# ScalarE loads column addresses in three places of a step (12, 8 and 8, then 12, 8 and 12); the first nodes' words come in parts, and the tail goes by tiles

## The chip, the cores and the metric

The kernel runs on one NeuronCore of a Trainium2 chip. The core has five engines that run their own instruction streams and wait for each other through semaphores: TensorE (PE; its weight loads are listed as PEld), VectorE (DVE), ScalarE (ACT), GpSimd (POOL) and SyncE (SP). Sixteen DMA engines move data; transfers are issued by POOL (here the gathers, with an index per partition), SP and ACT. The metric is the device time of one execution in microseconds (us), as the median of several runs.

## The reference

One message-passing layer of a graph network over 12,500 nodes of 128 numbers and 412,500 edges sorted by destination. Cut to what matters:

```python
f0, f1 = x0 @ W1_0e, einsum(x1, W1_1o)      # scaled; halves: features and self part
e0, e1 = feat0[src], feat1[src]             # 128 numbers of the source node, per edge
h = gelu(gelu(edge_attr_8 @ W_mlp1) @ W_mlp2)
w00, w01, w10, w11 = h @ Wp_00, h @ Wp_01, h @ Wp_10, h @ Wp_11
mid0 = [w00 * e0 * ea0,  w11 * sum(e1 * ea1)]
mid1 = [(w01 * e0) x ea1,  w10 * e1 * ea0]
n0, n1 = segment_sum(mid0, dst), segment_sum(mid1, dst)
y = c * self + s * [n0 @ W2_0e, n1 @ W2_1o]
out = layernorm(x + y)
```

## The kernel before

**Tiling.** The edges are cut into 806 runs of 512 (`SB`), one run to a step `s`; a run has four quarters of 128 edges (`Q`), one edge to a partition. Four steps are a chunk `c` (202 chunks). The nodes are cut into 25 groups of 512 (`GN`, the last has 212 nodes, in tiles of 128 and 84).

**Start** (the loop over `b`). x is loaded group by group (SP, tile `own`), turned by PE and copied by ACT into `xT` (x with the node number along the free axis, kept in SBUF), multiplied by `wf` and stored by ACT's queue to `table` in DRAM: `table` holds every node's features. The list `weight_loads()` is issued by SP, one entry in each turn of this loop from b = 5 on; before the change its last entries are `first_node` (the first destination of each chunk) and the tiles `tile_first` (shown as `tf` in the trace: the first destination of each of the 16 quarters of a chunk, 4-byte words, one row for each chunk; 128 rows in the first tile and 74 in the second, whose last row is loaded apart). `tile_places` (DVE) turns these words into byte offsets, which `places(c)` loads into PE's registers. After the loop SP issues `aid_load()`, up to 12 entries a step: the source numbers of the columns that are picked or aided (tiles `pick` and `aid_at`).

**A step.** The features of the 512 source nodes come into `G[s]` in three ways. Most quarters are fetched by POOL with one gather of 128 rows each (`gather`, L222). The last quarter of every 14th run is fetched by SP with 128 single-row transfers (`aid`). One quarter of some runs is *picked*: DVE or ACT copies 128 single columns out of `xT` into a tile `gt`, each copy with a column address out of a register (L190 on DVE, L192 on ACT), PE multiplies `gt` by `wf` (L198) and ACT writes the result into `G` (L199). How many columns an engine picks in a step, and in which places of the step, is the table `SLOTS`: DVE 12 and 12, with 0, 8, 8 or 16 more; ACT 12 and 16. `pick_nodes(e, s, slot)` loads that many addresses into registers (TENSOR_LOAD, L178), and `pick(e, n)` issues the copies of addresses that were loaded earlier. 172 quarters are picked by ACT, 197 by DVE and 56 are aided; POOL is left with 2,798 gathers, of which the first 72 read x itself.

With the edge weights `w` (PE, from the two-layer MLP whose gelus run on ACT, L540 and L556, in the odd steps of a chunk, two chunks ahead), DVE forms the messages `M` (L637 once and L641 twice a step), and PE sums them by destination with the one-hot tiles `own` (L666, L668) into `sums`. DVE adds `sums` to `acc` after each chunk (`add`). `select(c)` (DVE, ahead of each chunk) builds `own` and reads one value of each gathered quarter into `SEEN` (L597), so that DVE waits there for the gathers.

**Groups of nodes.** When all edges of a group are in `acc`, `moments` (PE L698 and L701, copy by ACT L706) computes its output rows, `statistics` (DVE, L714) their mean and variance, `normalise` (ACT L742) the result, and SP stores it. The last full group (`before_last`) falls due near the end, the last group after the last chunk.

**Order.** PE, ACT, DVE and SP run their instructions in the order in which the program writes them; POOL's gathers stand in the order of the steps. `G` has 19 buffers (`LEAD`), so a gather may be issued up to 18 steps ahead of its use. The transfers of SP and ACT take turns on eight semaphores; a transfer waits until the one before it on its semaphore has landed.

Of the kernel before, what the change touches and what calls it, by code (L numbers as in the profile page):

```python
# [21 lines left out]
P = 128  # L22
# [27 lines left out]
STEPS = 12  # L50
SLOTS = {DVE: [(12, 12, 0), (12, 12, 8), (12, 12, 8), (12, 12, 16)], ACT: [(12, 16)]}
COL_Q = {DVE: Q - 2, ACT: Q - 3}
COL_FROM = {DVE: 12, ACT: 12}
LNB = 2
TURN_AT = (7, 9, 11, 13, 15, 17, 18, 20, 22, 24)


@with_exitstack
def gnn_kernel(ctx: ExitStack, tc: tile.TileContext, x, src, dst, ea4, ea8, w1_0, w1_1, wm1, wm2,
# [277 lines left out]
    def weight_loads():  # L337

        yield w1r, sub(wm1, 0, [[0, P // RAD], [HID, RAD], [1, HID]])
        yield w2b, sub(wm2, 0, [[0, 2], [HID, HID], [1, HID]])  # L340
        for j, w in enumerate((wp00, wp01, wp10, wp11)):
            yield wpb[:, j * MUL:(j + 1) * MUL], sub(w, 0, [[0, 2], [MUL, HID], [1, MUL]])
        for t, w in ((w20, w2_0), (w21, w2_1)):
            yield t[:MUL, :], w[:MUL, :]
            yield t[MUL:, :], sub(w, MUL * MUL, [[0, 3], [MUL, MUL], [1, MUL]])
        yield first_node, sub(dst, 0, [[1, 1], [CH * SB, NCH]])
        for b, t in enumerate(tile_first):
            c0, n = b * P, t.shape[0]
            last = c0 + n == NCH and E < NCH * CH * SB
            if last:  # L350
                yield (t[n - 1:n, :].rearrange("a (k o) -> a k o", o=1),
                       sub(dst, (NCH - 1) * CH * SB, [[1, 1], [0, CH * Q], [1, 1]]))
                k = -(-(E - (NCH - 1) * CH * SB) // P)
                yield t[n - 1:n, :k], sub(dst, (NCH - 1) * CH * SB, [[k * P, 1], [P, k]])
            yield t[:n - last], sub(dst, c0 * CH * SB, [[CH * SB, n - last], [P, CH * Q]])

# [35 lines left out]
    first_at = cst.tile([1, NCH], I32)  # L392
    NT = -(-NCH // P)
    tile_first = [cst.tile([min(P, NCH - b * P), CH * Q], I32, name=f"tf{b}") for b in range(NT)]
# [12 lines left out]

    def tile_places():

        for b, t in enumerate(tile_first):  # L410
# [234 lines left out]
    def places(c):  # L645

        b, r = divmod(c, P)
        _, PLACE[c] = nc.values_load_multi_w_load_instructions(
# [35 lines left out]
    pend, done = [], []  # L684
    before_last = due[NCH - 1][0] - 1

    def moments(b, sums=None):
        n0, nn, full, tail, tiles = group(b)
        if not pend:
            Y["y"] = wk.tile([P, LNB, XB, P], F32, name="y", bufs=1)  # L690
            Y["v"] = wk.tile([P, LNB * XB, 2], F32, name="mv")
            nc.vector.memset(Y["v"], 1.0)
        j = len(pend)
        pend.append(b)
        pt = ps.tile([P, XB, P], F32, name="h")
        at = n0 - base[-1] if b in due[NCH - 1] else 0
        for t, k in tiles:
# [5 lines left out]
            else:  # L703
                nc.vector.tensor_tensor(pt[:k, t, :], pt[:k, t, :], sums[:k, t, :], op=OP.add)
        if full:
            nc.scalar.activation(Y["y"][:, j, :full, :], pt[:, :full, :], AF.Copy)  # L706
        if tail:
            nc.scalar.activation(Y["y"][:tail, j, full, :], pt[:tail, full, :], AF.Copy)

    def statistics(b):  # L710
        j = pend.index(b)
        st = wk.tile([P, XB, 6], F32, name="bst")
        for t, k in group(b)[4]:
            nc.vector.bn_stats(st[:k, t, :], Y["y"][:k, j, t, :])  # L714
            nc.vector.bn_aggr(Y["v"][:k, j * XB + t, :], st[:k, t, :])
# [7 lines left out]
    def normalise(last=False, keep=False):  # L723
# [9 lines left out]
        for j, b in enumerate(pend):  # L733
            if b in done:
                continue
            for t, k in group(b)[4]:
                i = j * XB + t - i0
                if last and t % 2:
                    nc.vector.tensor_scalar(y[:k, j, t, :], y[:k, j, t, :], r[:k, i:i + 1], m[:k, i:i + 1],
                                            op0=OP.mult, op1=OP.add)  # L740
                    continue
                nc.scalar.activation(y[:k, j, t, :], y[:k, j, t, :], AF.Identity,  # L742
                                     bias=m[:k, i:i + 1], scale=r[:k, i:i + 1])
            store_nodes(nc.sync, out, b, y[:, j])
        done[:] = pend if keep else []
# [3 lines left out]
    def norm(bs):  # L749
        for b in bs:  # L750
            moments(b)
            move_sums()
# [13 lines left out]
    def norm_last(bs):  # L766
# [6 lines left out]
        if len(pend) > len(done):  # L773
            deviations()
            normalise(True)

    odd_f = cst.tile([1, 1], F32)
# [118 lines left out]
    with tc.manual_schedule(engines={PE, ACT, DVE, SP}):  # L896
# [7 lines left out]
        for b in range(min(AHEAD, NG)):  # L904
# [41 lines left out]
        for s in range(NCH * CH + CH):  # L946
# [120 lines left out]
```

## Time and profile before

| | us |
|---|---|
| median of 3 runs (3550.64 to 3557.92) | 3552.09 |
| profiled execution, its own time | 3556.29 |
| its span in the profile | 3554.4 |

| engine | busy us | share of the span |
|---|---|---|
| PE | 3159.9 | 89% |
| DVE | 3129.2 | 88% |
| ACT | 2797.6 | 79% |
| POOL | 2667.6 | 75% |

The profile page gives the busy time of each engine, the chain of work that ended last, and groups of instructions by source line with the idle time ahead of them and what ended it. Busy time leaves out what an engine's sequencer does: address loads, semaphore waits and the issue of transfers (rows marked ACTq, DVEq, SPq). "issue" as the end of an idle stretch means that nothing else in the profile ended it. A row of the windows view gives a stretch of the span, its length, and then busy time and count of the chosen instructions in it.

### The profile page before, as it was taken

What the parts mean: (1) busy time and instruction counts of PE and PEld (TensorE: products, weight loads), DVE (VectorE), ACT (ScalarE), POOL (GpSimd) and SP (SyncE); (2) the same over time, 40 slices, a digit from 0 to 9 for tenths busy, and PEclk for the clock granted to TensorE, in tenths of its full rate; (3) what the DMA queues carried; (4) which work ended last, traced back from release to release, by engine and by line L of the source; (5) the groups of instructions that cost most, each with busy time, mean ns of one, the idle gap of its engine ahead of it and who ended that gap; (6) DMA issues with size and microseconds to landing.
All of it is one profiled execution on the core that took longest, in us unless ns stands there. A gap on an engine that the chain in (4) does not pass through costs nothing. (4 is left out here: it accounts for less than half of the span.)

```text
span 3554.4 us, 143693 instructions
## 1 busy us (share of the span) xinstructions
PE 3159.9 (89%) x28598; PEld 2755.6 (78%) x28598; DVE 3129.2 (88%) x29317; ACT 2797.6 (79%) x23671; POOL 2667.6 (75%) x2804
## 2 busy tenths in 40 slices
PE   6899898998898988998899898898899989888888
PEld 6777777787777777877788787787787777777777
DVE  2699999999999999999899899888899888889897
ACT  3488788788888888887887888877787887788785
POOL 7777777777777777777777777777777777777775
PEclk8999999998999999899998899989899999999998
DMA  8322332223322223322323323323323232232221
GB/s 199 70 62 68 63 64 65 63 61 74 64 60 67 63 60 74 64 60 62 68 61 70 67 59 64 65 63 68 65 62 64 59 69 63 60 69 63 60 65 47
DMA packets 579225, 239.29 MB, mean 67 GB/s; under 512 B 483651, under 2 KB 528747, under 8 KB 578347
## 3 DMA queue, kind: packets, MB, share of 16 engines
q0 software_dynamic: 89536, 183.55, 20.3%
q1 hardware_dynamic: 468041, 40.02, 9.1%
q10 hardware_dynamic: 20770, 6.47, 0.8%
q8 instruction: 252, 4.13, 0.5%
q14 instruction: 626, 5.13, 0.5%
HBM read 217.00 MB, written 12.80 MB: 65 GB/s over the span
## 5 line engine op out<-in xcount | busy, mean ns | idle before, releaser
L222 POOL DMA_INDIRECT G<-table,idx x2726 | 2598.9, 953 | 836.7 <-issue 718.5
L192 ACT ACTIVATE gt<-xT 128x1 f32 x22016 | 2166.7, 190 | 73.3 <-issue 53.6
L190 DVE COPY gt<-xT 128x1 f32 x25216 | 1728.6, 144 | 212.1 <-issue 172.9
L666 PE MATMUL sums<-own,M 128*128 128x96 f32 x6446 | 1354.8, 294 | 74.3 <-DVE M L641 73.0
L668 PE MATMUL sums<-own,M 128*128 128x96 f32 x6446 | 1319.7, 288 | 85.1 <-DVE M L641 84.1
L666 PEld LDWEIGHTS sums<-own,M 128*128 128x128 f32 x6446 | 1037.5, 201 | 181.9 <-DVE M L641 101.7
L668 PEld LDWEIGHTS sums<-own,M 128*128 128x128 f32 x6446 | 1035.3, 202 | 108.9 <-DVE M L641 107.6
L641 DVE TENSOR_TENSOR M<-w,G 128x384 f32<-128x384 f32 x1612 | 880.1, 547 | 0.0
L569 PE MATMUL w<-wpb,h 64*128 64x128 f32 x6448 | 649.3, 305 | 57.8 <-DVE M L641 56.3
L569 PEld LDWEIGHTS w<-wpb,h 64*128 64x128 f32 x6448 | 496.5, 197 | 199.6 <-issue 74.3
L637 DVE TENSOR_TENSOR M<-w,G 128x256 f32<-128x256 f32 x806 | 333.4, 414 | 34.4 <-issue 19.9
L540 ACT ACTIVATE h<-h 128x512 f32<-128x512 f32 x404 | 216.3, 586 | 178.6 <-PE h L536 165.7
L536 PE MATMUL h<-eT,w1b 64*128 64x128 f32 x3232 | 288.7, 319 | 8.4 <-ACT e L523 8.3
L536 PEld LDWEIGHTS h<-eT,w1b 64*128 64x128 f32 x3232 | 241.3, 218 | 38.7 <-ACT e L523 13.7
L556 ACT ACTIVATE h<-h 128x512 f32<-128x512 f32 x404 | 213.5, 577 | 26.3 <-PE h L551 22.5
L551 PE MATMUL h<-h,w2b 64*64 64x256 f32 x3232 | 222.6, 391 | 0.0
L199 ACT ACTIVATE G<-h 128x128 f32<-128x128 f32 x369 | 96.4, 277 | 120.5 <-PE h L198 76.4
L198 PE MATMUL h<-wf,gt 128*128 128x128 f32 x738 | 143.5, 294 | 1.9 <-ACT h L556 0.9
L529 ACT ACTIVATE eT<-h 128x128 f32<-128x128 f32 x202 | 56.0, 277 | 112.7 <-PE h L527 89.5
L551 PEld LDWEIGHTS h<-h,w2b 64*64 64x64 f32 x3232 | 104.5, 133 | 44.8 <-issue 0.5
L630 DVE TENSOR_TENSOR own<-oh,e 128x512 f32<-128x512 f32 x202 | 137.6, 681 | 0.7 <-issue 0.2
L681 DVE TENSOR_TENSOR acc<-sums,acc 128x384 f32 x202 | 111.2, 550 | 9.7 <-issue 6.2
(113 smaller groups left out, 1329.1 us busy)
## 6 DMA issues: line engine op xcount, KB each, us to landing
G<-table SPq DMA_DIRECT2D x7168, 0.5 KB
G<-table,idx POOLq DMA_INDIRECT x2726
e<-in_edge_attr SPq DMA_DIRECT2D x201, 64.0 KB
own<-in_x SPq DMA_DIRECT2D x24, 256.0 KB
table<-acc ACTq DMA_DIRECT2D x24, 256.0 KB
xt<-in_edge_attr SPq DMA_DIRECT2D x24, 256.0 KB
out<-y SPq DMA_DIRECT2D x24, 256.0 KB
xt<-in_dst SPq DMA_DIRECT2D x5, 256.0 KB
```

Of the source, the lines that this page charges most:

```text
L190: nc.vector.tensor_copy(to, col)
L192: nc.scalar.activation(to, col, AF.Copy)
L222: nc.gpsimd.indirect_dma_start(out=G[s][:, q, :], out_offset=None, in_=x if s < raw_runs else table, in_offset=bass.IndirectOffsetOnAxis(a ...
L536: nc.tensor.matmul(p1[h][:, j // 2, j % 2, :], w1b[rows, j, :], eT[c][rows, :], start=True, stop=True)
L540: nc.scalar.activation(H1[c][h], p1[h].rearrange("p k j e -> p (k j e)"), AF.Gelu_apprx_tanh, scale=1.0 / math.sqrt(RAD))
L551: nc.tensor.matmul(p2[r][k * HID:(k + 1) * HID, h * n:(h + 1) * n], w2b[rows, :], H1[c][h][rows, k * n:(k + 1) * n], start=True, stop=True)
L556: nc.scalar.activation(H2[c][r].rearrange("p k j e -> p (k j e)"), p2[r], AF.Gelu_apprx_tanh, scale=1.0 / math.sqrt(HID))
L569: nc.tensor.matmul(WP[i][:, q, :], H2[c][q % 2][rows, k, q // 2, :], wpb[rows, :], start=True, stop=True)
L637: nc.vector.tensor_tensor(M[s][:, :, :, :MUL], w[:, :, :2 * MUL].rearrange("p q (a u) -> p q a u", a=2), g[:, :, None, :MUL].to_broadcast( ...
L641: nc.vector.tensor_tensor(M[s][:, :, j, MUL:].rearrange("p q (i u) -> p q i u", i=3), w[:, :, None, (2 + j) * MUL:(3 + j) * MUL].to_broadc ...
L666: nc.tensor.matmul(flat[:, bass.ds(at, 4 * FIRST_HALF)].bitcast(F32), M[s][:, q, 0, :], own[:, 3 * WIDE:], start=False, stop=False)
L668: nc.tensor.matmul(sb[:, 1:, bass.ds(at, 4 * WIDE)].bitcast(F32), M[s][:, q, 1, :], own[:, :3 * WIDE].rearrange("p (a j) -> p a j", a=3), ...
```

## The change

**1. Three places for ACT's addresses.** ACT's row of `SLOTS` becomes (12, 8, 8) in one step and (12, 8, 12) in the next: 28 and 32 columns in turn, 30 on average, in place of 28. The third load stands behind a new `pick` that comes ahead of the gelus of the odd steps. With the larger number of columns 184 quarters are picked by ACT in place of 172, and POOL's gathers from `table` become 2,714 in place of 2,726.

**2. First nodes' words.** `tile_first` becomes three tiles that begin at chunks 0, 16 and 144. `first_node` and the first tile (16 rows) are loaded first in the list of SP; the other two tiles (128 rows, and 58 of which one is loaded apart) are loaded behind the pick rows, after the start loop. `tile_places` runs for the first tile in the start loop and for the other two in step 9.

**3. Tail by tiles.** Of the four tiles of `before_last`, three are computed by `moments` in earlier chunks, as soon as each is complete (`done_at`); `find_first` clamps the offsets of later sums so that they leave these tiles alone. The last group's rows stay in PSUM and are read there by `statistics` and `normalise`, without a copy by ACT, and its two tiles are stored each by its own transfer, one from ACT's queue and one from SP's.

```diff
-SLOTS = {DVE: [(12, 12, 0), (12, 12, 8), (12, 12, 8), (12, 12, 16)], ACT: [(12, 16)]}
+SLOTS = {DVE: [(12, 12, 0), (12, 12, 8), (12, 12, 8), (12, 12, 16)], ACT: [(12, 8, 8), (12, 8, 12)]}
+FIRST_TILES = 16
...
     def weight_loads():
+        yield first_node, sub(dst, 0, [[1, 1], [CH * SB, NCH]])
+        yield from tile_loads(0)
         yield w1r, sub(wm1, 0, [[0, P // RAD], [HID, RAD], [1, HID]])
...
-        yield first_node, sub(dst, 0, [[1, 1], [CH * SB, NCH]])
-        for b, t in enumerate(tile_first):
...
+    def tile_loads(b):
+        t, c0 = tile_first[b], tile_from[b]
+        n = t.shape[0]
...
+        yield t[:n - last], sub(dst, c0 * CH * SB, [[CH * SB, n - last], [P, CH * Q]])
...
+    tile_from = [0, *range(FIRST_TILES, NCH, P)]
...
+    done_at = [math.ceil((before_last * GN + (t + 1) * P + MARGIN) / N * NCH) - 1 for t in range(XB)]
...
     def find_first():
...
+        for t, (a, z) in enumerate(zip(done_at, done_at[1:])):
+            nc.vector.tensor_scalar(strays[:, a + 1:z + 1], strays[:, a + 1:z + 1], float((t + 1) * P), None, op0=OP.max)
...
-    def moments(b, sums=None):
+    def moments(b, sums=None, part=None):
         n0, nn, full, tail, tiles = group(b)
+        if part is not None:
+            tiles = tiles[part:part + 1]
...
+        if sums is None and b == NG - 1:
+            Y["pt"] = pt
+            return
+        if part is not None:
+            nc.scalar.activation(Y["y"][:, j, part, :], pt[:, part, :], AF.Copy)
+            return
...
+    def rows_of(b, j, t, k):
+        return Y["pt"][:k, t, :] if b == NG - 1 and "pt" in Y else Y["y"][:k, j, t, :]
...
+                if last:
+                    eng = nc.sync if t % 2 else nc.scalar
+                    eng.dma_start(out[b * GN + t * P:b * GN + t * P + k, :], y[:k, j, t, :])
...
-            moments(b)
+            moments(b, part=XB - 1 if b == before_last else None)
...
-                 NG // 2 + 9: tile_places, NG // 2 + 10: lambda: mlp2(1), NG // 2 + 11: make_ws, NG: make_wpost}
+                 NG // 2 + 9: lambda: tile_places([0]), NG // 2 + 10: lambda: mlp2(1), NG // 2 + 11: make_ws, NG: make_wpost}
...
-        late = list(aid_load())
+        late = list(aid_load()) + [load for b in range(1, NT) for load in tile_loads(b)]
...
+            pick(ACT, P)
+            pick_nodes(ACT, s, 2)
             if k % 2 and c + 2 < NCH:
-                pick(ACT, P)
                 (mlp1 if k == 1 else mlp2)(c + 2)
...
+            if k == 3 and c - 1 in done_at[:-1]:
+                moments(before_last, part=done_at.index(c - 1))
...
+            if s == 9:
+                tile_places(range(1, NT))
```

On ACT, an odd step and the step after it, in the steady part of the program (`gt` are picked columns, `pick` their addresses, `h` the two halves of a gelu). Before:

```order
L178 TENSOR_LOAD pick_832
L192 ACTIVATE gt_40310<-xT 128x1 x12
L178 TENSOR_LOAD pick_832
L192 ACTIVATE gt_40310<-xT 128x1 x16
L556 ACTIVATE h_40621<-h 128x512
L556 ACTIVATE h_40623<-h 128x512
L178 TENSOR_LOAD pick_832
L192 ACTIVATE gt_40310<-xT 128x1 x12
```

And now, with the change's line numbers (L179 is the load, L193 the copy):

```order
L193 ACTIVATE gt_44344<-xT 128x1 x12
L179 TENSOR_LOAD pick_823
L193 ACTIVATE gt_44344<-xT 128x1 x8
L179 TENSOR_LOAD pick_823
L556 ACTIVATE h_45433<-h 128x512
L556 ACTIVATE h_45435<-h 128x512
L193 ACTIVATE gt_44344<-xT 128x1 x12
L179 TENSOR_LOAD pick_823
```

Ahead of the two gelus of an odd step now stand 20 copies of that step in place of 28, with a load between the copies and the gelus, and 12 copies stand behind them.

On SP, the end of the start loop and the loads behind it (`own` are groups of x, `tf` the first nodes' words, `e` edge attributes). Before:

```order
L925 DMA tf_95<-in_dst 1x16x1
L252 DMA own_75<-in_x 128x128
L254 DMA own_75<-in_x 84x128
L925 DMA tf_95<-in_dst 1x7x1
L925 DMA tf_95<-in_dst 73x16x1
L496 DMA e_828<-in_edge_attr 128x16x8
L959 DMA aid_at<-in_src 56x128
L959 DMA pick_830<-in_src 128x128
L959 DMA pick_831<-in_src 69x128
L959 DMA pick_832<-in_src 19x128 x2
```

And now:

```order
L253 DMA own_75<-in_x 128x128
L255 DMA own_75<-in_x 84x128
L512 DMA e_819<-in_edge_attr 128x16x8
L993 DMA aid_at<-in_src 56x128
L993 DMA pick_821<-in_src 128x128
L993 DMA pick_822<-in_src 69x128
L993 DMA pick_823<-in_src 9x128 x8
L993 DMA pick_823<-in_src 8x128 x7
L993 DMA pick_824<-in_src 4x128 x11
L993 DMA pick_824<-in_src 3x128 x4
L993 DMA tf_95<-in_dst 128x16x1
L993 DMA tf_96<-in_dst 1x16x1
```

The words stand behind the pick rows now, and ACT's pick rows take 30 transfers in place of 14, since the pattern of picked runs repeats less often.

On PE, `before_last` between the last steps (`h` the group's rows, `sums` the messages' sums). Before:

```order
L668 REGISTER_ALU
L668 MATMUL sums<-own_74,M 128x3x32
L698 MATMUL h<-ws,xT 128x128
L701 MATMUL h<-wpost,acc 128x128 x4
L698 MATMUL h<-ws,xT 128x128
L701 MATMUL h<-wpost,acc 128x128 x4
L698 MATMUL h<-ws,xT 128x128
L701 MATMUL h<-wpost,acc 128x128 x4
L698 MATMUL h<-ws,xT 128x128
L701 MATMUL h<-wpost,acc 128x128 x4
L569 MATMUL w<-wpb,h_203822 128x128 x2
```

And now:

```order
L685 REGISTER_ALU
L685 MATMUL sums<-own_74,M 128x3x32
L717 MATMUL h<-ws,xT 128x128
L720 MATMUL h<-wpost,acc 128x128 x4
L585 MATMUL w<-wpb,h_209287 128x128 x2
```

Three of the four tiles have left this place; they stand six, four and two chunks earlier, one at each.

More of the change, by code (lines that the diff above doesn't have):

```diff
@@ L345, in weight_loads @@
             yield t[MUL:, :], sub(w, MUL * MUL, [[0, 3], [MUL, MUL], [1, MUL]])
[L346 to L355 removed]
+    def tile_loads(b):
+        t, c0 = tile_first[b], tile_from[b]
+        n = t.shape[0]
+        last = c0 + n == NCH and E < NCH * CH * SB
+        if last:
+            yield (t[n - 1:n, :].rearrange("a (k o) -> a k o", o=1),
+                   sub(dst, (NCH - 1) * CH * SB, [[1, 1], [0, CH * Q], [1, 1]]))
+            k = -(-(E - (NCH - 1) * CH * SB) // P)
+            yield t[n - 1:n, :k], sub(dst, (NCH - 1) * CH * SB, [[k * P, 1], [P, k]])
+        yield t[:n - last], sub(dst, c0 * CH * SB, [[CH * SB, n - last], [P, CH * Q]])
     def make_w1b():
@@ L392, in gnn_kernel @@
     first_at = cst.tile([1, NCH], I32)
-    NT = -(-NCH // P)
-    tile_first = [cst.tile([min(P, NCH - b * P), CH * Q], I32, name=f"tf{b}") for b in range(NT)]
+    tile_from = [0, *range(FIRST_TILES, NCH, P)]
+    NT = len(tile_from)
+    tile_first = [cst.tile([z - a, CH * Q], I32, name=f"tf{b}")
+                  for b, (a, z) in enumerate(zip(tile_from, tile_from[1:] + [NCH]))]
+    before_last = due[NCH - 1][0] - 1
+    assert len(due[NCH - 1]) == 1
+    done_at = [math.ceil((before_last * GN + (t + 1) * P + MARGIN) / N * NCH) - 1 for t in range(XB)]
+    assert due[done_at[-1]] == [before_last] and done_at == sorted(set(done_at))
+    assert not any(c in due for c in range(done_at[0] - 1, done_at[-1])) and done_at[-1] < NCH - 2
     def find_first():
@@ L406, in find_first, with tile_places @@
         nc.vector.tensor_reduce(odd[0:1, 2 * NB:2 * NB + 1], strays, axis=mybir.AxisListType.X, op=OP.add)
-    def tile_places():
-        for b, t in enumerate(tile_first):
+    def tile_places(bs):
+        for b in bs:
+            t = tile_first[b]
             n = t.shape[0]
@@ L645, in places @@
     def places(c):
-        b, r = divmod(c, P)
+        b = max(b for b, a in enumerate(tile_from) if a <= c)
+        r = c - tile_from[b]
         _, PLACE[c] = nc.values_load_multi_w_load_instructions(
@@ L692, in moments @@
             nc.vector.memset(Y["v"], 1.0)
-        j = len(pend)
-        pend.append(b)
+        if b not in pend:
+            pend.append(b)
+        j = pend.index(b)
         pt = ps.tile([P, XB, P], F32, name="h")
@@ L737, in normalise @@
                 i = j * XB + t - i0
+                z = rows_of(b, j, t, k)
                 if last and t % 2:
-                    nc.vector.tensor_scalar(y[:k, j, t, :], y[:k, j, t, :], r[:k, i:i + 1], m[:k, i:i + 1],
+                    nc.vector.tensor_scalar(y[:k, j, t, :], z, r[:k, i:i + 1], m[:k, i:i + 1],
                                             op0=OP.mult, op1=OP.add)
[L741 to L744, printed above, removed]
+                else:
+                    nc.scalar.activation(y[:k, j, t, :], z, AF.Identity,
+                                         bias=m[:k, i:i + 1], scale=r[:k, i:i + 1])
+                if last:
+                    eng = nc.sync if t % 2 else nc.scalar
+                    eng.dma_start(out[b * GN + t * P:b * GN + t * P + k, :], y[:k, j, t, :])
+            if not last:
+                store_nodes(nc.sync, out, b, y[:, j])
         done[:] = pend if keep else []
```

4 lines of the change are left out of this document (2 added, 2 removed).

## The prediction

> **What bounds the kernel now.** I read the page's groups first, for the engine that never rests, then the windows by steps, then the waits. The page shows GpSimd busy for only 75% of the span, but its row and the list of its first and last gathers tell another story:
>
> ```profile
> L222 POOL DMA_INDIRECT G<-table,idx x2726 | 2598.9, 953 | 836.7 <-issue 718.5
> L222 POOL DMA_INDIRECT G<-in_x,idx_raw x72: 940/944/1091, 3.8 to 92.7; - x72
> L222 POOL DMA_INDIRECT G<-table,idx x2726: 938/944/1508, 99.4 to 3528.3; - x195
> POOL G L222 <- issue: 740.2, 2427, 0.3
> POOL G L222 <- DVE M L641: 50.2, 147, 5.7
> ```
>
> Nearly every gather has 0.3 us ahead of it, whatever is named as its releaser (740.2 over 2427, 50.2 over 147): that gap belongs to the gather. The only long wait is one of 5.7 us near 99 us. GpSimd therefore issues gathers without a pause from 3.8 to 3528.3 us. What the steps do beside it (first the message instruction, one per step; then the gathers):
>
> ```profile
> 100.00:400.00 300.00, 28.69 (x70) 0.95 0.29 63
> 400.00:1900.00 1500.00, 147.27 (x356) 0.94 0.30 64
> 1900.00:3400.00 1500.00, 142.76 (x345) 0.93 0.30 64
> ...
> 400.00:1900.00 1500.00, 1136.18 (x1194) 0.94 0.30 64
> 1900.00:3400.00 1500.00, 1136.45 (x1193) 0.93 0.30 64
> ```
>
> The gathers run at the same pace in both halves: 1500/1194 = 1.256 us each. The steps do not: 1500/356 = 4.213 us, then 1500/345 = 4.348 us. In the first half the other engines use up GpSimd's head start; in the second they run at its heels, and DVE begins to wait for gathers. Of DVE's 45 us of such waits all but 4 lie after 1900 us:
>
> ```profile
> DVE SEEN L597 <- DMA G<-table,idx: 36.8, 32, 2.1
> DVE SEEN L597 <- DMA G<-table: 8.5, 10, 2.6
>   DMA G<-table: 4.1, 4
> ```
>
> (The last row is the part before 1900 us.) So the end is set by the number of gathers, and the other engines have 0.135 us a step in hand. What sets *their* 4.213 us is read between 300 and 1500 us, where they run free:
>
> ```profile
> 300.00:1500.00 1200.00, 1077.69 (x9931) 938.83 (x9930) 1105.93 (x10538) 995.76 (x8576) 909.05 (x955) 0.94 0.30 65
> DVE gt L190 <- issue: 60.3, 175, 0.6
> DVE M L637 <- PE w L569: 0.2, 1, 0.2
> PE sums L668 <- DVE M L641: 24.4, 35, 0.9
> ACT h L540 <- PE h L536: 39.1, 27, 5.6
> ```
>
> DVE is busy for 1105.9 of 1200 us and waits 60.3 us for its own address loads: 97% is its own. It waits for PE's weights once, 0.2 us; PE waits for DVE. ACT is busy for 995.8 us (83%) and mostly waits for PE.
>
> **Part 1, ACT's columns.** Twelve more quarters are picked, so twelve gathers go: 12 x 1.256 = **-15.1 us**, as long as GpSimd stays the bound. The price on ACT is two more copies a step:
>
> ```profile
> L192 ACT ACTIVATE gt<-xT 128x1 f32 x22016 | 2166.7, 190 | 73.3 <-issue 53.6
> L178 ACTq TENSOR_LOAD <-pick x1696: 306/808/1850, 143.9 to 3516.2; - x189
>   issue: 19.7, 84
> ```
>
> A copy costs 2166.7/22016 = 0.098 us, two of them 0.20 us a step, against an idle 0.72 us a step (204.2 of 1200 us, 285 steps). A third address load is sequencer time, 0.8 us as a median for 12 or 16 addresses; between 300 and 1500 us all loads together held ACT up for 19.7 us in 84 places, 0.07 us a step, so half as many again cost about 0.035 us (below: nothing; above: a whole 0.8 us each). ACT ends near 88% busy. None of this is on the path unless DVE comes to wait for PE and PE for ACT. PE does wait for gelus, 25.8 + 14.0 us in that window:
>
> ```profile
> PE h L527 <- ACT h L556: 25.8, 9, 5.4
> PE h L698 <- ACT h L556: 14.0, 8, 2.3
> ```
>
> The new order puts 8 copies fewer (0.79 us) ahead of the gelus in odd steps, which works against these waits. The cover is thin: the new bound gives a step (3509 - 95)/788 = 4.33 us on average over the table gathers, and over the whole run a free step may grow only from 4.213 to 4.25 before the saving shrinks (worked out under the rivals). I take -15.1; the bounds are in the rivals.
>
> **Part 2, first nodes' words.** The 5.7 us wait ahead of the first gather from `table` is named after DVE, but what is late is the table: ACT's last store is issued at 97.05. ACT had stood still for 10 us before:
>
> ```profile
> 71.02 0.60 ACT L295 ACTIVATE xT<-w 128x512 f32<-128x512 f32 x1 [0.26 <-PE w L294]
> 81.27 0.38 ACTq L260 DMA_DIRECT2D table<-acc  x1
> 81.75 1.08 ACT L540 ACTIVATE h<-h 128x512 f32<-128x512 f32 x2 [10.13 <-DMA pick<-in_src]
> 97.05 0.62 ACTq L262 DMA_DIRECT2D table<-acc  x1
> 99.37 0.94 POOL L222 DMA_INDIRECT G<-table,idx  x1 [5.68 <-DVE M L641]
> 65.16 1.58 SPq L925 DMA_DIRECT2D tf<-in_dst  x2
> 66.80 8.94 SPq L496 DMA_DIRECT2D e<-in_edge_attr  x1
> 76.87 11.40 SPq L959 DMA_DIRECT2D pick<-in_src  x16
> q1 hardware_dynamic: 1094, 0.00, 6.7%
> q1 hardware_dynamic: 2295, 0.12, 54.8%
> ```
>
> The store at 81.27 shares a semaphore with a pick load that SP could issue only after the 73 x 16 words: SP's next issue took 8.94 us, while its queue moved 1094 tiny packets in 9.2 us (66.8 to 76 us; the last row is the same queue at 59 to 62 us, where 2295 packets, most of them the words of the 128-row tile, took 3 us). The change takes this load out of the start, so ACT's 9.6 us go: its last store would come at 87.4. But now 33 pick loads stand ahead of the 128-row words, and by the program's semaphores the last two stores follow those. From about 63 us on, 33 x 0.71 us (11.40/16) gives 87, the words land near 91, the last store about 94, the gather at 95 to 96 in place of 99.37: **-4 us**. Bounds: the whole wait gone, -5.7; SP slower by a quarter or the words late, +4.
>
> [...] If the stall had another cause, this term would be nil and the sum -19.6 us.
>
> What goes elsewhere is small: `tile_places` for two tiles is twelve short DVE instructions in step 9, while GpSimd leads by some 16 steps.
>
> **Part 3, the tail.** From the start of the last gather 26 us pass. In them PE does four tiles of `before_last` in a row and DVE waits for the weights behind them:
>
> ```profile
> 3527.97 0.41 PE L698 MATMUL h<-ws,xT 128*128 128x128 f32 x2
> 3531.57 1.06 PE L701 MATMUL h<-wpost,acc 128*128 128x128 f32 x8
> 3532.56 0.71 PE L569 MATMUL w<-wpb,h 64*128 64x128 f32 x7
> 3536.21 0.42 DVE L637 TENSOR_TENSOR M<-w,G 128x256 f32<-128x256 f32 x1 [5.08 <-PE w L569]
> 3546.57 0.29 DVE L714 BATCH_NORM_STATS2 bst<-y 128x6 f32<-128x128 f32 x1 [1.94 <-ACT y L706]
> 3546.40 3.47 SPq L260 DMA_DIRECT2D out<-y  x2
> 3549.97 0.72 SPq L262 DMA_DIRECT2D out<-y  x1
> ```
>
> 3532.56 - 3527.97 = 4.59 us for four tiles; three leave: -3.4. DVE's 5.08 us are longer than that, so all of it counts. The earlier tiles cost PE 1.15 us each at places where it waits anyway. Without ACT's copy the statistics start about 0.5 us earlier, and two queues in place of one save some 0.6 us at the end (the second issue). **-4.5 us**; below -5.5, above -2 if earlier tiles push a step.
>
> **Sum:** -15.1 - 4 - 4.5 = -23.6 us. The profiled span of 3554.4 becomes 3530.8. The median of the runs, 3552.09, lies 2.3 us below that span; I subtract from it: **3528.5 us**.
>
> **Rivals.** (a) *The start gains nothing* because the last stores wait as long for the words behind 33 loads: 3532.5, or 3536.5 with the loss of 4. For it: more loads, same semaphores; against it: ACT's 9.6 us. (b) *ACT's work reaches DVE in part.* 72 steps are done at 400 us (2 before 100, 70 after); the last 734 take x each, and 15 us follow (3539 to 3554), 10.5 after the change. The new span is 400 + 734x + 10.5: it exceeds 3530.8 when x is over 4.251, and 3554.4 when x is over 4.283. With x = 4.263 (0.05 of the 0.20 us arrives): 3539.5, so 3537 as a median. (c) *Slower: ACT becomes the bound's feeder.* If half of the added work arrives at DVE, through late gelus or late picked quarters, x = 4.313: 3576, so **3574**; with all of it 3647. It decides from +0.07 us a step. For it: six times less slack than added work, and 19.7 us of exposed loads already. Against it: DVE waited for the weights for 0.2 us in 285 steps, PE has waits for DVE to give, and gelus come earlier. (d) *The change does not do what it says*: the twelve quarters fall in the free first half. That cannot save less, since the total number of gathers sets the last one.
>
> **Chances.** The forecast 0.65 (own range 3525 to 3534); (a) 0.13; (b) 0.10, half of it faster still and half level with before; (c) 0.12. A measurement of this kernel tells 0.2%, 7 us, from no change. Faster: 0.65 + 0.13 + 0.05 = 0.83; same 0.05; slower 0.12. Eight times in ten the time lies from 3520 to 3546: below the forecast for a start and tail at their bounds and the runs' spread, above it for (a) and most of (b).
>
> **What would show it.** Right: 2,714 gathers from `table` at 1.256 us; the first near 95 us and the last near 3509; steps at 4.2 us, then 4.33, with DVE's waits for gathers beginning later than 1900 us; ACT near 88% busy between 300 and 1500 us; one tile of L698's kind among the last steps and 21.6 us from the start of the last gather to the end. Wrong: a free step above 4.25 us, DVE waiting for `w`, or GpSimd waiting for a buffer by more than 0.3 us, would be (b) or (c); a first table gather at 99 us or later would be (a).

## The result: 66.6 ms in place of 3.55, and where the profile puts it

The changed kernel takes 66,644.89 us (median of 4 runs, 66,607.38 to 66,678.48) where the kernel before took 3555.01 us on the same chip: 18.75 times as long (95% interval 18.72 to 18.78). The forecast was 3528.5 us.

The page of the changed kernel begins like this (a group's columns: line, engine, operation, result and operand, count, then busy us, mean ns, and idle time ahead with what ended it):

```profile
span 66676.7 us, 678515 instructions
...
PEclk9955555555555555555555555555555555555555
...
L859 PE MATMUL h<-ident,g_a 125*8 125x125 f32 x3300 | 1213.9, 368 | 28287.2 <-DMA g_a<-in_edge_attr 28287.2
L918 POOL DMA_INDIRECT sums<-G,g_to x3300 | 3995.2, 1211 | 28442.0 <-DVE G L917 28442.0
...
L223 POOL DMA_INDIRECT G<-table,idx x2714 | 2587.9, 954 | 834.3 <-issue 652.0
```

Read the counts before the times. The 2,714 gathers of the forecast are there, with their 954 ns. The granted clock falls to about half after the first twentieth of the span (9 tenths, then 5), and the costliest groups occur 3,300 times, on lines that the prediction never named: 412,500 edges / 125. They belong to `general()`, the second path of the program, which computes everything again, 125 edges at a time, each pass waiting for its own transfers. The timeline of SP in the changed kernel shows where it starts (start, length, engine, line, transfer):

```profile
3535.15 0.35 SPq L775 DMA_DIRECT2D out<-y  x1
3536.38 21.57 SPq L261 DMA_DIRECT2D sums<-ft  x25
...
3559.78 0.29 SPq L844 DMA_DIRECT2D g_si<-in_src  x1
```

The fast path issues its last store at 3535.15 us, and then the general path begins. That leaves (66,676.7 - 3536.4)/3300 = 19.1 us a pass. The program enters it by this, at its very end:

```python
padded = P - RP if RP else 0                 # 44: empty places in the last quarter
n_odd = nc.values_load(odd_i, ...)           # edges and runs that don't fit the fast path
with tc.If(n_odd > padded):
    general()
```

`n_odd` counts, among others, edges whose destination lies below the first of their quarter, or 8 (`J`) or more above it. From the inputs the kernel before counts 44, the empty places alone, against a limit of 44: there is no margin, and a single odd edge more decides.

What changed the count shows in the transfers into the scratch tile (listed as `acc`), in the view of that tile on SP. Of the kernel before:

```profile
L480 SPq DMA_DIRECT2D acc<-in_dst x1: 659/659/659, 22.3 to 22.3; - x1
...
L925 SPq DMA_DIRECT2D acc<-in_dst x1: 646/646/646, 53.4 to 53.4; - x1
```

Of the changed kernel:

```profile
L496 SPq DMA_DIRECT2D acc<-in_dst x1: 647/647/647, 22.2 to 22.2; - x1
...
L959 SPq DMA_DIRECT2D acc<-in_dst x1: 812/812/812, 28.4 to 28.4; - x1
```

and, from its DVE timeline, the instruction that reads the first of them:

```profile
41.02 0.42 DVE L473 CAST ft<-acc 128x512 f32<-128x512 int32 x1
```

The first transfer brings the destinations of the first 128 runs (512 words a row, run 0 in row 0), the second brings `first_node`: `line(0, I32)`, the first 202 words of row 0 of the same tile. Before, it came at 53.4 us, after the words had been read (at 41.62 us there). Now it comes at 28.4 us and run 0's first 202 words are gone when DVE reads them at 41.02 us. The transfers and the read come in the order in which the program writes them, so this is no race: the program says it so. Counting run 0 again with those words: in its first quarter 127 of 128 are 8 or more above the first; in its second, 73 of 74 likewise, and the 54 that are left now lie below the first. 127 + 73 + 54 = 254, and 44 + 254 = 298 > 44.

### The profile page after: what moved, and what is told of

It is laid out like the page before. It is cut to its first block, busy times and chain, and to the rows that moved or that the text cites. A ratio compares the mean times of both kernels' runs of the same rounds, so it can differ in the third digit from the quotient of the medians.

```text
span 66676.7 us, 678515 instructions
## 1 busy us (share of the span) xinstructions
PE 25039.1 (38%) x101418; PEld 17416.0 (26%) x101418; DVE 17140.9 (26%) x92411; ACT 12800.6 (19%) x45159; POOL 14627.8 (22%) x12693
## 5 line engine op out<-in xcount | busy, mean ns | idle before, releaser
L918 POOL DMA_INDIRECT sums<-G,g_to x3300 | 3995.2, 1211 | 28442.0 <-DVE G L917 28442.0
L856 POOL DMA_INDIRECT G<-table,g_si x3300 | 3980.2, 1206 | 21579.7 <-DMA g_a<-in_edge_attr 20088.8
L894 PE MATMUL h<-wpost,G 128*125 128x128 f32 x26400 | 6834.3, 440 | 1554.0 <-ACT G L891 1554.0
L894 PEld LDWEIGHTS h<-wpost,G 128*125 128x125 f32 x26400 | 5854.0, 327 | 2505.5 <-ACT G L891 2505.5
L889 PE MATMUL w<-ident,G 125*128 125x125 f32 x13200 | 3522.0, 422 | 6216.3 <-DVE G L881 6216.3
L914 POOL DMA_INDIRECT G<-sums,g_di x3300 | 3995.7, 1211 | 1006.4 <-DVE G L876 949.7
L889 PEld LDWEIGHTS w<-ident,G 125*128 125x128 f32 x13200 | 2334.6, 216 | 7095.1 <-issue 7095.1
L877 DVE SCALAR_TENSOR_TENSOR G<-G,g_a 125x32 f32<-125x32 f32 x3300 | 830.8, 252 | 9179.0 <-ACT G L873 9179.0
L905 PE MATMUL h<-G 125*125 125x128 f32 x6600 | 2600.4, 496 | 1209.6 <-ACT G L896 1209.6
L871 PE MATMUL w<-wpb,G 64*125 64x128 f32 x6600 | 2599.2, 496 | 1184.2 <-ACT G L869 1184.2
L885 DVE SCALAR_TENSOR_TENSOR G<-G,g_a 125x32 f32<-125x32 f32 x9900 | 2443.3, 247 | 0.0
L883 DVE SCALAR_TENSOR_TENSOR G<-G,g_a 125x32 f32<-125x32 f32 x9900 | 2442.7, 247 | 0.0
```

What stands on the lines that cost most here:

```text
L856: nc.gpsimd.indirect_dma_start(out=g, out_offset=None, in_=table, in_offset=bass.IndirectOffsetOnAxis(ap=si, axis=0))
L871: nc.tensor.matmul(pw, h2, wpb[:HID, :], start=True, stop=True)
L883: nc.vector.scalar_tensor_tensor(m[:, 1 + k, :MUL], w[:, MUL:2 * MUL], a4[:, 1 + k:2 + k], g[:, :MUL], op0=OP.mult, op1=OP.mult)
L885: nc.vector.scalar_tensor_tensor(m[:, 1 + k, r], w[:, 3 * MUL:], a4[:, 1 + k:2 + k], g[:, r], op0=OP.mult, op1=OP.mult)
L889: nc.tensor.transpose(pm[:, k, :T], m[:, k, :], ident[:T, :T])
L894: nc.tensor.matmul(pc, mt[:, k, :T], wpost[:, k, :], start=k == 0, stop=k == 3)
```

## The experiments: what sets off the general path

The theory is the overwrite, with a count of exactly 298. The rivals: the clamp that part 3 adds to `find_first`, or the split tiles of part 2, raise the count. The four kernels ran on one chip, where the kernel before took 3552.63 us (9 runs, 3551.96 to 3555.68).

**A limit of 298.**

```diff
-    with tc.If(n_odd > padded):
+    with tc.If(n_odd > padded + 254):
```

> The changed kernel with one constant other: the branch into the general path asks whether the count of odd edges and runs exceeds 298 instead of 44. Theory (the overwrite): first_node is now loaded before the destinations of run 0 are read out of the same words, so run 0 has 202 wrong destinations; from the inputs the count is 44 + 54 + 200 = 298, so the branch is not taken and the time is that of the fast path alone: 3540 us (3533 to 3546), 11 to 15 us under the kernel before. Run 0's messages go to wrong nodes here, and nothing repairs them. Rivals (the clamp of the later sums, or the places of the three tiles, is counted as odd): the clamp covers up to 198 chunks and the tiles up to 202 x 16 words, so the count could be any number; over 298 the time is 66.6 ms.

Measured: 3535.77 us (4 runs, 3531.38 to 3541.86), ratio to the kernel before 0.9956 (0.9941 to 0.9971).

**A limit of 297** (`padded + 253`).

> As the run with the limit of 298, but with 297. The overwrite gives a count of exactly 298, so here the general path runs and the time is 66.6 ms. If the count is any other number under 298, both runs are fast; over 298, both slow. Only a count of exactly 298 separates them.

Measured: 66,692.21 us (one run). The count is over 297 and not over 298: exactly the number from the inputs.

**The kernel before with the load moved.**

```diff
     def weight_loads():
+        yield first_node, sub(dst, 0, [[1, 1], [CH * SB, NCH]])
...
-        yield first_node, sub(dst, 0, [[1, 1], [CH * SB, NCH]])
```

> The kernel before, with one line moved: the load of first_node stands first in weight_loads instead of ahead of the tiles. Nothing else of the change is in it: no clamp, two tiles as before, the old tail and SLOTS. The overwrite: 66.6 ms (the fast part of 3.55 ms and 63.1 ms of the general path). The clamp or the tiles as the cause: 3552 us, as before.

Measured: 65,845.94 us (one run), and the general path's groups stand in its page:

```profile
L825 PE MATMUL h<-ident,g_a 125*8 125x125 f32 x3300 | 1214.1, 368 | 27644.8 <-DMA g_a<-in_edge_attr 27644.8
```

One moved line in the kernel before is enough; neither clamp nor split is in it. That its general path is 0.8 ms shorter than the changed kernel's was not followed up.

**The change with other words for `first_node`.**

```diff
-    first_node = line(0, I32)
+    first_node = line(12, I32)
```

> The changed kernel with one constant other: first_node lies in line 12 of the scratch tile, words that no early load writes, instead of line 0. All three parts of the change stay, and the load stays early. The overwrite: the count is 44, the branch is not taken, 3540 us (3533 to 3546). The clamp or the tiles as the cause: still 66.6 ms. Where the time of the fast part goes: first gather from the table near 94 us, GpSimd waits of about 6 us in all at 160 to 190 us, last gather near 3514.6, and 25 us from there to the end. The prediction's own sum (3528.5) would need the waits at 160 to 190 us away and a tail shorter by 4.5 us.

Measured: 3540.59 us (5 runs, 3533.24 to 3541.87), ratio 0.9960 (0.9947 to 0.9974). With everything else of the change in place the general path is gone. The overwrite is the cause, and the clamp and the split are not.

## The experiments: the terms of the sum

This last version, called the mended kernel from here on, is the one that the prediction's sum was about. Its gathers, in the view of their line:

```profile
L223 POOL DMA_INDIRECT G<-table,idx x2714: 940/944/1500, 94.5 to 3507.9; - x194
```

Its windows by DVE's message instruction, one a step:

```profile
400.00:1900.00 1500.00, 148.02 (x357) 0.95 0.28 64
1900.00:3400.00 1500.00, 144.22 (x348) 0.94 0.27 64
```

by the gathers:

```profile
400.00:1900.00 1500.00, 1136.72 (x1192) 0.95 0.28 64
```

and by engine (PE, PEld, DVE, ACT, POOL):

```profile
300.00:1500.00 1200.00, 1084.78 (x9913) 944.38 (x9912) 1106.00 (x10525) 1046.50 (x9118) 909.35 (x954) 0.94 0.28 65
```

A gather still takes 1500/1192 = 1.258 us and a free step 1500/357 = 4.20 us (in the second half 1500/348 = 4.31, forecast 4.33), although ACT is now busy for 1046.5 of 1200 us (87%; the forecast said near 88%). First gather from the table at 94.5 us (forecast near 95), last at 3507.9 (near 3509), span 3531.5 (3530.8). What the expectation had from the changed kernel's own trace, 6 us of waits at 160 to 190 us and 25 us behind the last gather, was not there: one wait of 1.0 us and one of 0.6, and 23.6 us.

That agreement is partly luck. The profiled execution of the kernel before took 3556.29 us, above most of its runs; that of the mended kernel took 3533.24, the fastest of five. The two kernels without the general path (limit 298, and line 12) have nine runs from 3531.4 to 3541.9 us with a median of 3536.4: 16 us below the 3552.6 of the kernel before, not 23.6. One possible source of their spread shows in the changed kernel's own trace, whose fast path executes the same instructions. Windows of it, of the run with the limit of 298, and of the mended kernel, from 150 to 165 us (PE, PEld, DVE, ACT, POOL busy; then the granted clock):

```profile
150.00:165.00 15.00, 12.17 (x74) 10.44 (x75) 6.62 (x60) 7.80 (x56) 10.56 (x12) 0.66 0.28 60
```

```profile
150.00:165.00 15.00, 11.99 (x105) 10.70 (x103) 8.87 (x82) 9.81 (x78) 11.31 (x12) 0.96 0.27 60
```

```profile
150.00:165.00 15.00, 11.97 (x116) 10.05 (x114) 10.04 (x95) 9.90 (x77) 11.34 (x13) 1.00 0.27 61
```

The first had a clock of 0.66 there, and PE completed 74 matmuls in place of 116 in about the same busy time. In these steps raw rows are still turned by PE and GpSimd is as far ahead as its buffers allow, so it comes to wait. Its timeline in the changed kernel:

```profile
166.75 0.94 POOL L223 DMA_INDIRECT G<-table,idx  x1 [2.83 <-ACT gt L193]
...
172.12 0.94 POOL L223 DMA_INDIRECT G<-table,idx  x1 [1.93 <-issue]
...
180.65 0.94 POOL L223 DMA_INDIRECT G<-table,idx  x1 [1.34 <-DVE M L657]
```

With one more wait near 191 us these cost 6.1 us beyond the usual 0.3 us a gather, for good: its last gather starts at 3514.6 us. The mended kernel's profile has one such wait, of 1.0 us, near 170 us, and one of 0.6 us near 187; so has that of the limit of 298.

No rest of PE sets the three apart: its longest from 100 us to the dip is 2.08 us in all of them. From 110 to 154 us PE, DVE and ACT run the same instructions in the changed and the mended kernel, 1.30 us apart, and only one clock then drops. In the clock's records of the changed kernel the clock is 1.0 or 0.5 between 100 and 3500 us, each time for 3.41 us or a whole multiple of it; so it is in those of the kernel before. The stretch near 150 us in which PE works least, and the next one, in the changed kernel (PE busy; then the clock):

```profile
151.20:154.62 3.42, 1.49 (x11) 1.00 0.48 58
154.62:158.03 3.41, 3.41 (x20) 0.50 0.24 69
```

with the limit of 298:

```profile
144.43:147.84 3.41, 1.33 (x12) 1.00 0.21 59
147.84:151.25 3.41, 3.41 (x19) 0.50 0.21 59
```

and in the mended kernel:

```profile
152.79:156.20 3.41, 1.77 (x14) 1.00 0.53 76
156.20:159.61 3.41, 3.08 (x29) 1.00 0.19 51
```

After 1.49 and 1.33 us of work the clock falls, after 1.77 it does not. Counted from the clock's records of the changed kernel, from 100 to 3500 us, it falls 63 times, with PE busy for at most 0.66 of the 3.41 us ahead of a fall; of the 37 such stretches at full clock with PE busy for under half, 35 were followed by half the clock. In the kernel before it falls 67 times, after at most 0.71, and 35 of 38 were followed by it. With PE busy for 0.45 to 0.66 both occur in either trace, so they give no sharp limit. In the changed kernel the half clock stays for 10.24 us (and 6.83 us more from 171.7 us), with the limit of 298 for 3.41 us, which cost GpSimd no wait that the mended kernel lacks. In the mended kernel the stretch begins 152.79 - 151.20 - 1.30 = 0.29 us later in the program than in the changed one, and PE is busy in it for 0.28 us more. That this decides about the dip is an estimate from these two traces alone; nothing else was run for it.

Whether the runs near 3541 us are the ones with such a dip stays open, since only the profiled executions have a trace. The mean clock of the mended kernel's runs doesn't tell (0.942 at 3541.87 us, 0.934 at 3534.43), but 10 us at half the clock change a mean over 3530 us by under 0.002.

**Each part alone, and 32 columns.** To price the terms, each part was put on the kernel before, in runs f1 (addresses), f2 (words, with line 12) and f3 (tail). Run f4 took all parts, with line 12 and with 32 columns in every step:

```diff
-... ACT: [(12, 8, 8), (12, 8, 12)]}
+... ACT: [(12, 8, 12)]}
```

> The kernel before with part 1 alone: ACT's row of SLOTS and the third place. By the prediction: 12 gathers fewer at 1.256 us, so 3537.5 us (15.1 under the kernel before). Its rival (b): ACT's added work reaches DVE in part, 3545 us or more. If the new order (12 + 8 + 8 copies ahead of the gelus) also delays the turning of raw rows in steps 10 to 17, GpSimd, which leads by 18 steps there, loses up to 6 us between 160 and 200 us, and the time is 3543 us; the profile then shows these waits although the first words are loaded as before.

> The kernel before with part 2 alone, first_node in line 12 of the scratch tile so that the general path is not taken. By the prediction 4 us less (bounds 5.7 less to 4 more): 3548.6 us. By the trace of the changed kernel the first table gather starts 5 to 5.6 us earlier; if nothing gives that back, 3547 us; if steps 10 to 17 end no earlier than before, whatever the start, GpSimd waits for buffers about as long between 160 and 200 us and the time is 3552 us.

> The kernel before with part 3 alone (two tiles of words as before, loads where they were). By the prediction 4.5 us less: 3548.1 us, and 21.6 us from the start of the last gather to the end. By the profile of the changed kernel with first_node in its own place, that stretch is 23.6 us against 26.1 before, so 2.5 us less: 3550 us. Rival: the earlier tiles push steps near the end, 3552 us or more.

> All three parts with first_node in line 12, and 12, 8 and 12 addresses in every step (32 columns, 196 quarters in place of 184, so about 12 gathers fewer again). If GpSimd still sets the end: 15.1 us under the version with 30 columns (3540.6), so 3525.5 us. If the step of the other engines (4.21 us while free) is by now as long as GpSimd's share of a step (4.31 us) plus what ACT's work at 91% busy adds, no gain or a loss: 3540 us or more, with GpSimd waiting for buffers and DVE no longer waiting for gathers.

None of these numbers came: these runs, and all later ones, fell on four other chips, on which the kernel before itself took 5522 to 5602 us. The runs of addresses alone and of 32 columns were repeated twice (g and h), all four once more (k), and at last the mended kernel ran beside 32 columns (m).

> Part 1 alone once more, because the first time all kernels (the kernel before too: 5532 us) ran on a chip where every engine paused between instructions and GpSimd was busy for 47%, so that no gather could set the end. If the kernel before is at 3552 us here: 3537.5 us by the prediction's 12 x 1.256 us, 3543 us if the order of part 1 makes GpSimd wait between 160 and 200 us, 3545 us or more if ACT's work reaches DVE.

> All three parts, first_node in line 12, 32 columns in every step, once more for the same reason. If the kernel before is at 3552 us here: 3525.5 us if GpSimd still sets the end (12 gathers fewer than with 30 columns), 3540 us or more if the steps of the other engines do, with GpSimd waiting for buffers.

> Part 1 alone a third time, since on both chips so far every engine paused between instructions (the kernel before 5532 and 5590 us), and GpSimd's gathers could not set the end. If the kernel before is at 3552 us: 3537.5 us by 12 x 1.256 us, 3543 us if GpSimd waits 6 us between 160 and 200 us, 3545 us or more if ACT's work reaches DVE. If it is at 5500 us or more again: 0.5% slower, as twice before.

> All three parts, first_node in line 12, 32 columns in every step, a third time. If the kernel before is at 3552 us: 3525.5 us if GpSimd still sets the end, 3540 us or more if the steps of the other engines do. If it is at 5500 us or more again: 2.3% faster, as twice before.

> Part 1 alone, on a chip where the kernel before takes 3552 us: 3537.5 us by 12 x 1.256 us; 3545 us or more if ACT's work reaches DVE. If the kernel before is at 5500 us or more: 0.4 to 0.5% slower, as on the two chips before.

> Part 2 alone (first_node in line 12). If the kernel before is at 3552 us: 3547 us, since the first table gather starts 4.8 us earlier in the version with all parts and GpSimd waits only 1 us of it again where TensorE's granted clock stays at 1.00 in steps 10 to 17; 3552 us if that clock dips there (0.66 in the profile of the changed kernel, with 8 us of waits).

> Part 3 alone. If the kernel before is at 3552 us: 3550 us, by the 2.5 us that the tail is shorter in the version with all parts; 3548 us by the prediction; 3552 us or more if earlier tiles push steps.

> All three parts, first_node in line 12, 32 columns in every step. If the kernel before is at 3552 us: 3525.5 us if GpSimd still sets the end, 3540 us or more if the steps of the other engines do. If it is at 5500 us or more: 2.3% faster, as on the two chips before.

> The mended change (first_node in line 12, 30 columns) again, beside 32 columns in the same call. If the kernel before is at 3552 us: 3537 us (3533 to 3542, as before). If it is at 5500 us or more: 0.5% slower, as part 1 alone was; if it comes out 2% faster instead, as 32 columns did, then it is the three parts together and not the step from 30 to 32 columns that helps on such a chip.

> 32 columns with all three parts, in the same call as the mended change. If the kernel before is at 3552 us: 3525.5 us if GpSimd still sets the end, 3540 us or more if the steps of the other engines do. If it is at 5500 us or more: 2.4% faster.

| kernel | median us | the kernel before, beside it | ratio (95% interval) |
|---|---|---|---|
| addresses alone, f / g / h / k | 5555.4 / 5616.9 / 5613.4 / 5549.1 | 5531.9 / 5590.4 / 5590.7 / 5522.5 | 1.0049 (1.0034-1.0065) / 1.0046 (1.0031-1.0062) / 1.0038 (1.0023-1.0054) / 1.0055 (1.0036-1.0075) |
| words alone, f / k | 5523.2 / 5521.3 | 5531.9 / 5522.5 | 0.9985 (0.9971-0.9999) / 0.9993 (0.9976-1.0011) |
| tail alone, f / k | 5532.2 / 5528.5 | 5531.9 / 5522.5 | 1.0006 (0.9993-1.0020) / 1.0011 (0.9994-1.0028) |
| mended change, m | 5621.1 | 5601.5 | 1.0040 (1.0025-1.0056) |
| 32 columns, f / g / h / k / m | 5390.8 / 5467.2 / 5459.5 / 5379.3 / 5467.0 | 5531.9 / 5590.4 / 5590.7 / 5522.5 / 5601.5 | 0.9754 (0.9737-0.9772) / 0.9776 (0.9753-0.9800) / 0.9764 (0.9736-0.9791) / 0.9752 (0.9728-0.9776) / 0.9766 (0.9743-0.9788) |

Why these chips can't price the terms is read from the groups of one and the same kernel, the mended one. On the first chip:

```profile
L223 POOL DMA_INDIRECT G<-table,idx x2714 | 2585.8, 953 | 829.7 <-issue 655.5
L193 ACT ACTIVATE gt<-xT 128x1 f32 x23552 | 2320.2, 192 | 61.0 <-issue 45.6
```

and on one of the others:

```profile
L223 POOL DMA_INDIRECT G<-table,idx x2714 | 2567.4, 946 | 2885.7 <-issue 1426.1 <-DVE M L657 519.2 <-ACT h L572 309.8
L193 ACT ACTIVATE gt<-xT 128x1 f32 x23552 | 2536.9, 192 | 1326.4 <-issue 1311.6 <-DVE M L657 2.2 <-DMA G<-table 0.8
```

The durations are the same (953 and 946 ns, 192 and 192 ns); what grows is idle time ahead of the instructions that nothing in the profile ends. GpSimd now waits for DVE and ACT, so gathers no longer set the end there. The addresses alone cost 0.4 to 0.6% and the mended change 0.4%. Which part of the edit costs it, the two more copies a step or their new places, was not tried. The words save 0.15 and 0.07% there (one interval excludes no change, the other doesn't), the tail nothing that can be told.

The exception is 32 columns: 2.2 to 2.5% faster on all four chips, with more copies still, so the number of copies alone can't be what costs. In run m it and the mended change ran side by side, and the step from 30 to 32 columns alone is worth 5621.1 - 5467.0 = 154 us. Its groups on that chip:

```profile
L193 ACT ACTIVATE gt<-xT 128x1 f32 x25216 | 2686.0, 192 | 1247.0 <-issue 1233.3 <-DMA G<-table 1.1
L223 POOL DMA_INDIRECT G<-table,idx x2701 | 2563.6, 949 | 2706.1 <-DVE M L657 1067.9 <-issue 950.5 <-ACT h L572 365.9
```

Its 1,664 further copies come with 79 us less idle time ahead of ACT's copies. 32 columns are a quarter of 128, so a picked quarter is complete after exactly four steps, always at the same place; with 30, and with the 28 of before, it ends at a different place each time. Whether that is the reason stays open, and so does what 32 columns do on a chip where gathers set the end. By its medians it is the one version that beat the kernel before on every one of these chips, and the mended change on the one where both ran.

## Why the prediction was wrong

**The step that failed** is in part 2 and its rival. The prediction costed the moved loads as time only ("What goes elsewhere is small"), and of the rival "The change does not do what it says" it considered picked quarters alone, dismissed it ("That cannot save less") and left it no chance. Which words the moved transfer writes, who reads them after it, and the branch that counts odd edges were never worked out, though `first_node` was known to be moved ahead of everything in SP's list of weights. What the runs showed in its place: the moved load overwrites 202 words that are still to be read, the count becomes 298 against a limit of 44, and the general path adds some 63.1 ms; with other words for `first_node` the time is 3540.59 us. The mechanism is a data-dependent branch with a limit equal to the count: 44 against 44. No row of the profile of before shows it, because a path that isn't taken leaves no row. It shows in the code and the inputs only.

**Point by point, on the mended kernel's profile against that of the kernel before** (span 3531.5 against 3554.4):

- *Addresses, -15.1.* 2,714 gathers at 1.258 us (forecast 1.256), the free step 4.20 against 4.21 us: ACT's added work reached nobody there, and neither rival (b) nor (c) came. Where gathers don't set the end the sign turns: +0.4 to +0.6%. The condition "as long as GpSimd stays the bound" was in the text, but a chip on which it doesn't hold was not among the cases.
- *First words, -4.* The first table gather starts 99.37 - 94.54 = 4.8 us earlier. Of this 0.7 us is given back in the wait near 170 us, and 6.1 us were given back in the changed kernel's own trace, with the clock at 0.66. The size was right where the clock stayed; the prediction had no term for what it does to a GpSimd that is already as far ahead as its buffers allow. Of the mechanism half came. ACT's 10.13 us of waiting for a pick load did not go but shrank, and its last store was issued at 91.7 us in place of 97.05 (forecast about 94). From the ACT and POOL timelines of the mended kernel, and its queue of SP's transfers from 95 to 97 us:

```profile
78.03 0.60 ACT L604 ACTIVATE G<-h 128x512 f32<-128x512 f32 x1 [4.61 <-DMA pick<-in_src]
81.20 1.09 ACT L572 ACTIVATE h<-h 128x512 f32<-128x512 f32 x2 [2.08 <-DMA pick<-in_src]
91.68 0.58 ACTq L263 DMA_DIRECT2D table<-acc  x1
94.54 0.94 POOL L223 DMA_INDIRECT G<-table,idx  x1 [1.17 <-DVE M L657]
q1 hardware_dynamic: 983, 0.01, 27.6%
```

  The third tile's words came faster than the 73 rows had: in the last row nearly all packets are its 57 x 16 = 912 words, 983 in 2 us, about four times the pace of 1094 in 9.2 us, and the packets took 27.6% of the time of the 16 DMA engines in place of 6.7%. What slowed the 73 rows no run shows. Nothing of the sum hung on it.
- *Tail, -4.5.* From the start of the last gather to the end: 3531.5 - 3507.9 = 23.6 us against 26.1, so -2.5 us. Up to the start of the last message it is 2.5 us shorter (8.1 against 10.6), where the three PE tiles left and DVE's wait for the weights is 1.97 us in place of 5.08; the prediction had -3.4. After the last message nothing is gained, 15.5 us against 15.5. The statistics do come 0.4 us earlier, but the last normalisation on DVE now waits for that on ACT, which it didn't. Last rows of the mended kernel:

```profile
3525.57 0.46 ACT L771 ACTIVATE y<-h,rs 128x128 f32<-128x128 f32 x1 [1.03 <-DVE rs L760]
3526.05 0.37 ACTq L775 DMA_DIRECT2D out<-y  x1
3526.06 0.41 DVE L768 TENSOR_SCALAR y<-h,rs 84x128 f32<-84x128 f32 x1 [0.53 <-ACT y L771]
3526.49 0.36 SPq L775 DMA_DIRECT2D out<-y  x1
```

  and of the kernel before:

```profile
3548.93 0.34 DVE L739 TENSOR_SCALAR y<-y,rs 84x128 f32<-84x128 f32 x1
3548.99 0.49 ACT L742 ACTIVATE y<-y,rs 128x128 f32<-128x128 f32 x1 [1.09 <-DVE rs L732]
```

  Both now read the last group's rows in one PSUM tile; that this tile is what serialises them wasn't tried. The last stores are issued 0.44 us apart, and from the last issue to the end pass 5.0 us, against 4.4.
- *From a span to a median.* The prediction subtracted 2.3 us, as for the kernel before. Between two profiles the gain was 22.9 us; between the medians it was 12 and 17 us, in the two kernels without the general path.

The profiled gain is thus -15.1 - 4.8 + 0.7 - 2.5 = -21.7 of -22.9; the remaining 1.2 us lie in a slightly quicker pace of 2,714 gathers and are not explained. A single profile is no finer than that. The run with the limit of 298, whose fast path executes the same instructions, divides its 24.8 us otherwise: first gather 4.0 us earlier, 19.4 us less from the first to the last, and a tail shorter by 1.5 us (24.6 against 26.1).

## What to carry to other kernels

A load that is moved ahead of others is first a question of which words it overwrites and who still reads them, and only then one of time: here the transfers and the read kept the program's order, and a tile that serves two purposes gave wrong words without any race. Where a kernel ends in a branch on a count, work out that count and its limit from the inputs before costing anything, since a path that is not taken has no rows. And a saving on the bounding engine holds only where that engine is the bound: ask what the same change costs where it is not.

## What the runs showed of the hardware that had not been expected

On four of the five chips on which the experiments ran, the engines paused between instructions. The ACT timeline of addresses alone on one of them:

```profile
1501.62 0.30 ACT L192 ACTIVATE gt<-xT 128x1 f32 x2 [0.20 <-issue]
1502.35 0.30 ACT L192 ACTIVATE gt<-xT 128x1 f32 x2 [0.44 <-issue]
1503.08 1.08 ACT L556 ACTIVATE h<-h 128x512 f32<-128x512 f32 x2 [0.43 <-issue]
1504.05 0.39 ACT L192 ACTIVATE gt<-xT 128x1 f32 x3
1505.26 2.18 ACT L192 ACTIVATE gt<-xT 128x1 f32 x21 [0.82 <-issue]
```

Copies of 0.1 us each come in twos and threes, with 0.4 to 0.8 us of rest between them, and then 21 in a row. In the mended kernel's trace there, ACT's copies that wait for nothing start over 0.3 us after the copy ahead 1,933 times, against 224 on the first chip, and most of these distances are 0.6 to 0.8 us or 1.2 to 1.45 us (1,235 and 371). DVE shows the same (1,578 against 126), and the granted clock is 0.73 there against 0.94. What holds the instructions back no row shows, and it stays open. The lower clock need not be the cause: there PE is busy for 75% of the span in place of 89%, and on the first chip the clock fell after 35 of the 37 stretches of 3.41 us in which PE had worked for under half (the changed kernel's trace).

The fall of the clock is the other thing. In three executions of the same instructions it came near 150 us for 10.24 us, for 3.41 us and not at all, and on a kernel whose gain is 16 us GpSimd's waits behind the longest, from 163 to 191 us, made 6.1 us.
